# Statistics ahead of fusion's additions, no weight pieces in the fourth tile's slot, sequence 1 turned a slot later

## The chip, the cores and the metric

The kernel runs on one core of one Trainium2 chip. The metric is the device time of one execution in microseconds (us); lower is better. A kernel's time is the median of its runs. The engines are PE (TensorE: matmuls and transposes), PEld (its weight loads), DVE (VectorE), ACT (ScalarE), POOL (GpSimd) and SP (SyncE, which issues most DMAs). Each works through its own queue of instructions and waits on semaphores for the others.

## The reference: what is computed

`x` has 8 sequences of 512 tokens with 512 features, float32. A two-direction stack of four gated linear recurrences with layernorms, a fusion matmul of both directions, a residual, and a feed-forward block with ternary weights and a second residual:

```python
def _mingru(x, Wz, bz, Wh, bh):                  # here Wz and Wh are the same matrix, ctx[i]
    z = sigmoid(x @ Wz.T + bz)
    h_tilde = tanh(x @ Wh.T + bh)
    a = clip(1.0 - z, 1e-8, 1.0 - 1e-8)
    return linear_scan(a, z * h_tilde)           # h[t] = a[t] * h[t-1] + b[t], along the tokens

def _stack(x, ...):                              # 4 layers
    h = x
    for i in range(4):
        h_new = _mingru(h, ...)
        if i > 0:
            h_new = h_new + h
        h = layernorm(h_new) * gamma + beta
    return h

def _L0_xcond_ref(x, ...):
    h_fwd = _stack(x, ...)
    h_bwd = flip(_stack(flip(x), ...))
    return concat(h_fwd, h_bwd) @ fusion_W.T + fusion_b

def _L0_ffn_ref(x, ...):
    h = gelu(x @ absmean(W_fc).T)                # weights rounded to -1, 0, 1 by their mean size
    return (layernorm(h) * ln_w + ln_b) @ absmean(W_proj).T

x = x + _L0_xcond_ref(layernorm(x), ...)
x = x + _L0_ffn_ref(layernorm(x), ...)
```

## The kernel before

**Tiling and stages.** Features lie on the 128 partitions in `NC_` = 4 chunks (index `o` or `c`), tokens along the free axis; a tile is 128x512. Tokens are also cut into `NT` = 4 tiles of 128 (index `t`). The sequences are worked in four pairs (0,1), (2,3), (4,5), (6,7); a state is named by sequence and direction: (0,0), (0,1), (1,0), (1,1). A pair goes through a first layer (`first_layer`, both directions from one matmul), layers 1 to 3 (`layer`) and the fusion (`fusion`). The first layer of the next pair is woven into the fusion of this one. When all pairs are through, the feed-forward block (L747 on) runs over the eight sequences.

**Slots set the order.** The program is written in slots (`slot`, L407). A slot emits one piece of matmul work, then work that has become due, and counts `now` up by one. In a slot stand, in order: the matmuls (`work()`), the `factors` that are due, shares of the queued layernorm work (`shares`, L243, and `x_shares`), the `scans` that are due (clip L452, product L453, two scans L457), the rest of the slot's own work (`end()`), the `resid` work that is due, and last the parts of the shares that run on ACT. With `long=True`, used for the fusion tiles, `scans` and `end()` stand ahead of the shares. Within each engine the instructions keep this order.

**The layernorm between layers** (`norm`, L325) takes a token tile at a time: four transposes of 128x128 into a PSUM tile `pt` (L301; `ps_t` has two buffers), statistics on DVE (`stats`, L153: bn_stats, bn_aggr and two small operations), a power on POOL (L163), and on ACT the factor `nmr` (L173) and the normalised tile `tok` (L174), whose end frees `pt`. When the four `tok` of a state are there, `back` (L305) turns them back chunk by chunk into `pf` (two buffers) and ACT writes the new state (L316). `norm`'s argument `pause` says how many slots after the scans the first transposes come, `pair` how many go into a slot. In layer 3 (`norm_last`) only the statistics are made, and bn_stats frees `pt`.

**The fusion** (`fusion`, L535) of one token tile: DVE adds the bias `fb` to the row (L545), weight pieces are taken (`pieces`, L546), eight matmuls go into two PSUM tiles `pu` (L551; `ps_u` has four buffers, shared with `u`), and in `end()` DVE scales and adds both to the row (L559) and SP stores it (L562).

**Weight pieces.** `extra` is a list of small jobs: sums of absolute weights on ACT, the ternary weights `fcq` and `pwq` on DVE (`ternary`, L176: two operations a piece, L178 and L179), and four operations for the tile `comb` (L624 and L625). `pieces(n)` takes the next `n` of them; each piece's load is issued on SP up to three pieces ahead. They are spread over layers (L526) and fusion tiles (L546).

## Time and profile before

| | |
|---|---|
| median of 3 runs | 1749.28 us (1748.78 to 1749.43) |
| the profiled execution | 1748.87 us, its span 1746.9 us |
| mean granted TensorE clock | 0.994 of full speed |
| fusion's additions (L559) | 64, median 750 ns |
| bn_stats of a transposed tile (L156) | 256, mean 693 ns |
| scan (L457), forms `z` | 224, mean 1224 ns |
| first matmul of a first layer | 11.8 us |
| fusion of pairs 0 to 3 | from 274, 579, 884 and 1192 us |
| feed-forward block | from 1251 us |

The span runs from the first to the last instruction; the execution's time has 2.0 us more around it. A line of the timeline is: start, duration, engine, source line, operation, output<-inputs, sizes and count, and in brackets how long the engine had been idle before and what it waited for. A line of the waits is: who waited for whom, the total in us, how often, the longest. A line of a stretch is: its bounds, its length, the busy time of PE, PEld, DVE, ACT and POOL with the number of instructions, the granted clock, the share of the DMA engines and their GB/s.

### The profile page before, as it was taken

To read this page: it belongs to the slowest core of one execution; us is meant where nothing else is said; L and a number is where in the kernel's file an instruction comes from. 1 tells how busy PE (TensorE), PEld (TensorE's weight loads), DVE (VectorE), ACT (ScalarE), POOL (GpSimd) and SP (SyncE) were. 2 spreads that over 40 slices of the span, in tenths; PEclk is the share of its full clock that TensorE was granted. 3 is DMA by queue.
4 is the path that set the end of the run, shared out by engine and by line. 5 is a ranking of instruction groups with operands and counts; after the bars stand their busy time and mean duration, and the time that the engine had idled before them with its cause. 6 is when DMAs were issued, how large, how long until landed. Compare 5 with 4: busy or idle time off the path is not lost.

```text
span 1746.9 us, 19727 instructions
## 1 busy us (share of the span) xinstructions
PE 1713.6 (98%) x6424; PEld 1043.8 (60%) x6424; DVE 1453.2 (83%) x2865; ACT 1067.8 (61%) x1836; POOL 217.1 (12%) x334
## 2 busy tenths in 40 slices
PE   8899999999999989999999999999999999999998
PEld 4455554455555445555544555554588888888887
DVE  7889989779998987999898799997468778768876
ACT  3788873358886235888623588871256556565654
POOL 2011111111111111111111111111000000000000
PEclk9999999999999999999999999999999999999999
DMA  7002321150000125000012301101301101101100
GB/s 265 13 25 78 103 80 48 61 192 1 1 7 24 49 67 193 1 1 7 25 49 66 109 1 49 73 1 43 127 0 49 42 7 49 49 1 49 49 19 31
DMA packets 46454, 91.73 MB, mean 53 GB/s; under 512 B 5264, under 2 KB 5264, under 8 KB 45328
## 3 DMA queue, kind: packets, MB, share of 16 engines
q1 hardware_dynamic: 45488, 88.91, 15.1%
q10 hardware_dynamic: 864, 1.57, 0.3%
q8 instruction: 50, 0.82, 0.2%
q14 instruction: 52, 0.43, 0.1%
HBM read 65.30 MB, written 25.17 MB: 52 GB/s over the span
## 4 chain that ended last, share of the span: by engine, by line
PE 72%; DVE 21%; issue 4%; ACT 2%; POOL 0%; DMA 0%; DVEq 0%; POOLq 0%; ACTq 0%
PE u L429 27%; PE ph L790 12%; PE po L817 11%; PE pu L551 9%; DVE z L457 5%; PE pt L301 4%; PE pf L310 4%; DVE st L156 3%; DVE z L453 2%; PE u L472 2%; DVE zf L457 1%; DVE a L452 1%; DVE xf L559 1%; DVE mv L158 1%; PE py L199 1%
## 5 line engine op out<-in xcount | busy, mean ns | idle before, releaser
L429 PE MATMUL u<-h,gw 128*128 128x512 f32 x768 | 345.5, 593 | 0.0
L429 PE MATMUL u<-xT,gw 128*128 128x512 f32 x768 | 345.4, 593 | 0.0
L457 DVE TENSOR_TENSOR_SCAN z<-a,z 128x512 f32<-128x512 f32 x224 | 274.2, 1224 | 7.6
L794 ACT ACTIVATE g<-ph 128x512 f32<-128x512 f32 x128 | 76.4, 597 | 242.1 <-PE ph L790 242.1
L429 PEld LDWEIGHTS u<-h,gw 128*128 128x128 f32 x768 | 138.8, 190 | 139.1 <-issue 138.6
L429 PEld LDWEIGHTS u<-xT,gw 128*128 128x128 f32 x768 | 138.7, 190 | 139.1 <-issue 138.2
L446 ACT ACTIVATE a<-u,ngb 128x512 f32<-128x512 f32 x192 | 131.6, 685 | 141.4 <-PE u L429 140.8
L163 POOL TENSOR_TENSOR rs<-ve,mhalf 128x1 f32<-128x1 f32 x192 | 123.5, 643 | 736.4 <-DVE nmu L167 679.1
L156 DVE BATCH_NORM_STATS2 st<-pt 128x6 f32<-128x512 f32 x256 | 177.3, 693 | 33.4 <-PE pt L301 33.2
L817 PE MATMUL po<-pwq,ghi 128*128 128x512 f32 x512 | 203.6, 398 | 0.0
L790 PE MATMUL ph<-yhi,fcq 128*128 128x512 f32 x512 | 199.8, 390 | 0.0
L817 PE MATMUL po<-pwq,glo 128*128 128x512 f32 x512 | 199.7, 390 | 0.0
L790 PE MATMUL ph<-ylo,fcq 128*128 128x512 f32 x512 | 199.5, 390 | 0.0
L453 DVE TENSOR_TENSOR z<-z,t 128x512 f32<-128x512 f32 x224 | 153.4, 685 | 8.7 <-ACT z L448 8.6
L174 ACT ACTIVATE tok<-pt,nmr,rs 128x512 f32<-128x512 f32 x192 | 149.2, 777 | 6.4
L805 DVE TENSOR_TENSOR acc<-acc,g 128x512 f32<-128x512 f32 x112 | 77.3, 691 | 87.9 <-ACT g L794 87.0
L448 ACT ACTIVATE z<-u,gb 128x512 f32<-128x512 f32 x192 | 132.2, 688 | 0.0
L447 ACT ACTIVATE t<-u,gb 128x512 f32<-128x512 f32 x192 | 130.7, 681 | 0.7 <-DVE z L453 0.6
L301 PEld LDWEIGHTS pt<-ident,z 128*128 128x128 f32 x640 | 78.8, 141 | 80.5 <-issue 49.0
L173 ACT ACTIVATE nmr<-nmu,rs 128x1 f32<-128x1 f32 x192 | 56.7, 295 | 103.7 <-POOL rs L163 101.2
L551 PE MATMUL pu<-fw,xT 128*128 128x512 f32 x256 | 119.6, 611 | 0.0
L310 PE MATMUL pf<-ident,tok 128*128 128x128 f32 x768 | 113.5, 273 | 2.5 <-ACT tok L174 2.3
(138 smaller groups left out, 2621.0 us busy)
## 6 DMA issues: line engine op xcount, KB each, us to landing
xn<-in_x_dram SPq DMA_DIRECT2D x32, 256.0 KB, 4.6
xf<-in_x_dram SPq DMA_DIRECT2D x32, 256.0 KB, 5.5
x<-xf SPq DMA_DIRECT2D x32, 256.0 KB, 2.0
xy<-x SPq DMA_DIRECT2D x32, 256.0 KB, 3.7
out_dram<-xy SPq DMA_DIRECT2D x32, 256.0 KB, 2.0
xT<-in_xt_dram SPq DMA_DIRECT2D x7, 1024.0 KB, 7.3
fca<-in_fc_wT_dram SPq DMA_DIRECT2D x16, 256.0 KB, 2.9
pwa<-in_proj_wT_dram SPq DMA_DIRECT2D x16, 256.0 KB, 2.7
```

What stands on the lines that cost most here:

```text
L156: nc.vector.bn_stats(st, src)
L174: nc.scalar.activation(dst, src, AF.Identity, bias=nmr, scale=rs)
L301: nc.tensor.transpose(pt[:, ts(c, P)], zs[c][:, ts(t, P)], ident)
L310: nc.tensor.transpose(pf[:, ts(t, P)], toks[t][:, ts(c, P)], ident)
L429: nc.tensor.matmul(u, lhsT=gw[l][:, c, ts(o, P)], rhs=h[:, c, :], start=(c == 0), stop=(c == NC_ - 1),)
L446: nc.scalar.activation(a, u, AF.Sigmoid, bias=ngb[:, l, o : o + 1], scale=-1.0)
L448: nc.scalar.activation(z, u, AF.Sigmoid, bias=gb[:, l, o : o + 1])
L453: nc.vector.tensor_tensor(z, z, t, ALU.mult)
L457: nc.vector.tensor_tensor_scan(dst[:, d], a[:, d], z[:, d], 0.0, ALU.mult, ALU.add)
L551: nc.tensor.matmul(pu, lhsT=hs[d][:, c, ts(t, P)], rhs=fw[:, d * NC_ + c, :], start=(c == 0), stop=(c == NC_ - 1),)
L790: nc.tensor.matmul(ph, lhsT=w, rhs=ys[b][c][i], start=(c == 0 and i == 0), stop=(c == NC_ - 1 and i == 1),)
L817: nc.tensor.matmul(po[b][t], lhsT=part[:, ts(t, P)], rhs=pwq[k // NP_][:, k % NP_, :], start=(k == 0 and i == 0), stop=(k == NF - 1 and i ...
```

## The change

Four edits. In a `long` slot only the due `scans` stand ahead of the shares; `end()`, with fusion's two additions, now follows them as in any other slot. The last two slots of the first layers of sequences 0 and 1 become `long`. Both directions of sequence 1 wait two slots, not one, from the end of their first layer's scans to their transposes. And the pieces are dealt out differently: a fusion tile took 1, 2, 1, 2 of them; now the even sequence of a pair takes 1, 2, 1, 0 and the odd one 2, 2, 2, 2, as many in all. The four `comb` operations, which came in the four slots of state (6,0) in layer 3, now come in those of (6,1).

```diff
@@ slot
             if long:
                 due("scans")
-                end()
-                end = None
             last = shares(cap) + x_shares()
             due("scans")
             if end is not None:
@@ first_layer
-                                norm((b, 0), zf, f"{b}0_0", 1, 2 if b < 2 else 1)
+                                norm((b, 0), zf, f"{b}0_0", 2 if b == 1 else 1, 2 if b < 2 else 1)
...
-                                    norm((b, 1), zb, f"{b}1_0", 1, 2 if b < 2 else 1)
+                                    norm((b, 1), zb, f"{b}1_0", 2 if b == 1 else 1, 2 if b < 2 else 1)
@@ layer
-                if s[0] < 2 and (l == L - 1 or o % 2) and len(extra) > 2 * NW or s[0] + 2 >= B and l == L - 1:
+                if s[0] < 2 and (l == L - 1 or o % 2) and len(extra) > 2 * NW or s == (B - 2, 1) and l == L - 1:
                     pieces(1)
@@ fusion
-                    pieces(1 + t % 2)
+                    pieces((1, 2, 1, 0, 2, 2, 2, 2)[t + (b % 2) * NT])
@@ the calls of the first pair's first layers
         for i, work in enumerate(f0 + f1):
-            slot(work, 4 if i == NC_ + 1 else 2)
+            slot(work, 4 if i == NC_ + 1 else 2, i > NC_ + 1)
```

## The prediction

> **What bounds the kernel now.** First the page: how full the engines are. Then the waits of PE, then its timeline around each long wait, and last the stretches of time with their clock.

> ```profile
> span 1746.9 us, 19727 instructions
> PE 1713.6 (98%) x6424; PEld 1043.8 (60%) x6424; DVE 1453.2 (83%) x2865; ACT 1067.8 (61%) x1836; POOL 217.1 (12%) x334
> ...
> PE pt L301 <- ACT tok L174: 12.9, 8, 3.9
> PE pt L301 <- DVE zf L457: 3.9, 1, 3.9
> PE pf L310 <- ACT tok L174: 2.3, 4, 1.4
> PE pt L301 <- DVE st L156: 2.1, 6, 0.6
> ```

> PE decides the time and is idle for 33.3 us. The waits (total, times, longest) put most of it in a few places: one of 3.9 us on the last scan of sequence 1's first layer, and three of 3.9 us on a `tok`, one per fusion stage of the first three pairs. Pair 1's, in order of time:

> ```profile
> 628.53 3.60 PE L472 MATMUL u<-xT,gw 128*128 128x512 f32 x8
> 636.00 1.11 PE L301 MATMUL pt<-ident,zf 128*128 128x128 f32 x4 [3.87 <-ACT tok L174]
> 636.91 5.73 PE L551 MATMUL pu<-fw,xT 128*128 128x512 f32 x8
> ...
> 626.15 0.75 DVE L179 SCALAR_TENSOR_TENSOR fcq<-fcb,hi_fc,fcq 128x512 f32<-128x512 f32 x1
> 627.33 0.75 DVE L179 SCALAR_TENSOR_TENSOR fcq<-fcb,hi_fc,fcq 128x512 f32<-128x512 f32 x1
> 631.46 1.58 DVE L559 SCALAR_TENSOR_TENSOR xf<-pu,rsv,xf 128x512 f32<-128x512 f32 x2
> 632.95 0.69 DVE L156 BATCH_NORM_STATS2 st<-pt 128x6 f32<-128x512 f32 x1
> 634.10 0.69 DVE L156 BATCH_NORM_STATS2 st<-pt 128x6 f32<-128x512 f32 x1
> 635.17 0.78 ACT L174 ACTIVATE tok<-pt,nmr,rs 128x512 f32<-128x512 f32 x1
> ```

> The third transpose `pt` (two buffers) waits until ACT has read the first. That `tok` waits for the statistics, and DVE takes those up only at 632.95, though their `pt` stood ready by 628.3: ahead of them in its queue were two weight pieces (L178 and L179, 625.63 to 628.00), a product and two scans, and fusion's two additions (L559). The stretches show what a long wait costs besides (PE busy, PEld, DVE, ACT, POOL, then the granted clock):

> ```profile
> 631.97:636.00 4.03, 0.16 (x1) 0.00 (x0) 3.56 (x11) 1.09 (x3) 1.10 (x2) 0.80 0.41 130
> 636.00:642.47 6.47, 6.47 (x13) 3.17 (x13) 5.07 (x11) 4.07 (x7) 0.95 (x1) 0.60 0.12 43
> 1151.93:1154.00 2.07, 0.66 (x5) 0.42 (x4) 2.04 (x3) 1.29 (x3) 0.66 (x1) 1.00 0.00 0
> ```

> After a wait of 3.9 us the clock is 0.60 for 6.5 us: eight matmuls that take 3.43 us elsewhere take 5.56 (636.91 to 642.47). After the 1.4 us wait of the last pair it stays 1.00. At the start of the kernel:

> ```profile
> 46.32 0.70 DVE L156 BATCH_NORM_STATS2 st<-pt 128x6 f32<-128x512 f32 x1 [3.07 <-PE pt L301]
> 67.42 1.22 DVE L457 TENSOR_TENSOR_SCAN zf<-a,z 128x512 f32<-128x512 f32 x1
> 68.70 1.33 PE L301 MATMUL pt<-ident,zf 128*128 128x128 f32 x5 [3.88 <-DVE zf L457]
> ```

> DVE stands idle for 3.07 us before 46.32, for a transpose, with scans queued behind; 20 us later PE waits for just such a scan.

> [...] the four waits of 3.87 and 3.88 us are followed by slow matmuls, those of 1.41 us and less are not. [...] the ready statistics sat behind the additions. So position in the queue is the whole of this change. [...] Here 1224 ns against 685 for the product; two scans are the largest item moved at the start.

> **The change, part by part.** The order of instructions on each engine shows the same counts on every engine. PE's and ACT's order changes only between the end of `u_00_1_3` and the first matmuls of layer 1 of sequence 1. DVE's changes there, in the fusion slots, and in the last layer of the last pair; POOL's nowhere; on SP only three stores of x1 per pair move by a few places.

> *Fourth tile of fusion, three pairs.* DVE after the tile's addition of `fb` (ends 625.63) does no piece: clip, product and two scans, 3.46 us (628.00 to 631.46 before), end at 629.09; statistics at 629.09 and 630.24 (1.15 apart, as before), then the additions. From the start of the statistics to the end of `tok` is 3.00 us (632.95 to 635.95), so `tok` ends at 632.09. PE is through with its matmuls at 631.97 and loses 0.17. Before, it lost 10.50 (631.97 to 642.47) less 3.87 of work: 6.63; in pairs 0 and 2, 5.63 (326.77 to 336.27) and 5.62.

> *The pieces come back in the next slots* (two instead of one in tile 0 of the odd sequence; in tiles 1 and 2 two each). In that slot, after `st` for the third transpose (633.47 to 634.62), DVE does `fb` 0.60, two pieces 2.37, scans 3.46, and starts the next two statistics at 641.05 and 642.19; their `tok`s end at 644.0 and 645.14 (2.95 each, as at 646.83 to 649.78). PE, now ahead, asks for those buffers at 643.76 and 644.5: it waits 0.3 and 0.7, together 1.0, where it lost 0.31. That is 0.65 to 0.7 given back per pair. One slot on, the pieces hide under 6.87 us of fusion matmuls and a 0.12 us wait goes. The additions come 2.3 us later, ending at 632.9; the matmul that reuses their PSUM buffer starts at 636.0, so nothing waits, and 3 us of slack are left. In the last tile of the odd sequence they leave a DVE wait (2.68 us before 679.25) that covers their 1.5.

> *Tiles 0 and 2 of the even sequence.* There bn_stats alone frees `pt`; before, the third transpose waited 0.17 and 0.41 for it (pairs 1 and 2 only), plus 0.06 on each restart. With statistics first: 0.7 per pair saved.

> Pairs: 5.63-0.17-0.65+0.12 = 4.9; 6.63-0.17-0.65+0.12+0.7 = 6.6; pair 2 likewise 5.6. Sum 17.2 us.

> *The start.* With scans ahead of statistics, the clip, product and two scans of chunk 0 (3.45 us) run at 43.17 to 46.62, in the idle stretch. Statistics slip by 0.30, and PE with them once (`pf` at 51.42). DVE is 3.1 us ahead from then on; the last `zf` scan ends near 65.8 instead of 68.65. With pause 2 PE does not need it until 71.5: `pfold` and `u_01_1_0` (3.43 each) go first. Behind them come three slots in a row with two statistics each, without the 3.43 us of `pfold` between. Following DVE (2.3 for two statistics, 2.92 for clip to residual) and ACT (1.85 factors, 1.05 a `tok`, 0.7 an evacuation) slot by slot, I get PE waits of 0.65, 0.9 and 0.9, and 0.3 after. Before, between 64.33 and 99.68, PE lost 4.62 to the first transposes, 2.37 to the slow `pfold` and 0.78 in short waits: 7.8. After: 0.3+0.65+0.9+0.9+0.3 = 3.1. Gain 4.7. This term is the least sure: two engines are nearly full there (DVE 18.38 and ACT 19.05 of 20 us from 80 to 100). Bounds: 2 (waits doubled) and 7 (none).

> *Last pair.* The four `comb` pieces (1.8 us: 0.32, 0.58, 0.32, 0.60) leave sequence (6,0), and one of 0.32 precedes the statistics whose `tok` PE waited for (1.41 us). They start 1.5 earlier, at 1149.18; the wait goes, and the moved pieces add 0.1 at the next `ylo`. Gain 1.5. The FFN's statistics of `y` only profit. In fusion of sequence 6 the statistics wait for the transpose ahead of an addition that was ready, and DVE has idle time of 2.7 us per tile for it: nothing.

> The sum is 4.7+17.2+1.5 = 23.4 us. The profiled execution took 1748.87 (span 1746.9 and 2.0 around it), 0.4 below the median of 1749.28; so 1725.9, or 1726.

> **The rivals.** *B, the wait moves on.* DVE was busy nearly without a break from 625 to 643; if its lag in the slot with the two returned pieces is larger than I have it, or the start's three slots queue up, part returns as short waits: 2.5 us more per pair and 2 at the start give 1736. For it: the slack there is below 1 us. Against: DVE had 11.2 us of idle from 620 to 680, and 6.6 go.

> *C, the low clock isn't due to the wait.* Then the slow matmuls stay: 8.4 us (2.37, 1.13, 2.13, 1.12, and 0.25 plus three times 0.47 in transposes), 1734. Against: the clock is 1.00 in every stretch without such a wait.

> *D, it does not do what it says:* something else, such as ACT's turn for `tok`, held the fourth tile's slot. Then only the start's and the small gains stay, 6, and are used up by the added waits: about 1746 to 1752. Against: ACT was idle 11.0 us before that `nmr`.

> *E, slower.* Two slots in a row with two pieces, and x1 stores waiting on later additions ahead of the piece loads in SP's queue. If DVE falls 2.5 us further behind, [...] the clock falls again: about 6.5 us, at two places a pair, 39 in all against 23: 1765. [...] Against: the pieces needed are loaded a slot (8 us or more) ahead, where SP's loads landed in 2.9 us.

> **How the numbers follow.** As above 0.66 (own range 1721 to 1731), B 0.13, C 0.08, D 0.06, E 0.07. Range 1720 to 1736: below, no waits at all at the start and in the pairs; above, B and C. About 0.2% (3.5 us) is what can be told from no change. D splits over the three signs: faster 0.89, same 0.04, slower 0.07.

> **What would show it.** PE has no wait of 3.9 us after 60 us; the clock is 1.00 in the slices that had less; the `tok` of the fourth tile ends within 0.3 us of PE's last matmul; two waits near 0.3 and 0.7 us follow one slot later; before 46.6 DVE's idle of 3.07 is gone; PE's busy time falls by some 8 us and its idle time by 15. A wait above 3 us anywhere in fusion, or a clock below 1.00 there, would make it wrong.

## The result and the profile after

| | before | after |
|---|---|---|
| median of the timed runs | 1749.09 us (4 runs, 1748.78 to 1749.43) | 1724.88 us (4 runs, 1724.32 to 1725.23) |
| ratio, 95% interval | | 0.9861 (0.9844 to 0.9878) |
| span of the profiled execution | 1746.9 us | 1723.0 us |
| PE busy, PE idle | 1713.6, 33.3 us | 1704.6, 18.4 us |

24.2 us were gained, 23.4 forecast. The page of the kernel after, its span and how full the engines are:

```profile
span 1723.0 us, 19728 instructions
PE 1704.6 (99%) x6424; PEld 1039.2 (60%) x6424; DVE 1452.1 (84%) x2865; ACT 1067.0 (62%) x1836; POOL 214.6 (12%) x334
```

PE lost 14.9 us of idle time, and for the same 6424 matmuls 9.0 us of busy time. That fits the matmuls that ran at a granted clock of 0.50 before: PE was busy for 17.4 us there, and at 1.00 the same work would take half of that, 8.7 (an estimate from the granted clocks). DVE's work is the same. PE's waits (total, times, longest):

```profile
PE pt L301 <- ACT tok L174: 4.3, 11, 0.6
PE pm L669 <- DMA gw<-in_gru_wT_dram: 5.0, 1, 5.0
```

The line for `zf` is gone. The longest wait on a `tok` is 0.6 us, where it was 3.9. The 5.0 us is the first load, as before. (After line 413 every line number is two lower than before; in the experiments it is off by a few lines too.) The stretches, whose first number after the engines' busy times is the granted clock:

```profile
60.00:80.00 20.00, 19.41 (x58) 9.25 (x57) 19.09 (x38) 13.43 (x26) 1.75 (x3) 1.00 0.09 27
...
620.00:640.00 20.00, 19.06 (x62) 9.33 (x61) 18.91 (x45) 11.94 (x21) 4.09 (x6) 1.00 0.33 106
...
940.00:960.00 20.00, 20.00 (x69) 10.50 (x68) 15.63 (x25) 7.36 (x11) 0.55 (x1) 1.00 0.35 118
```

All are at 1.00. What is left of the places of the forecast stands in PE's timeline: the start, the fourth tile of pair 1 and the slot behind it, and the last pair.

```profile
76.65 0.66 PE L301 MATMUL pt<-ident,zf 128*128 128x128 f32 x4 [0.59 <-ACT tok L174]
77.14 3.60 PE L427 MATMUL u<-h,gw 128*128 128x512 f32 x8
...
617.02 3.60 PE L470 MATMUL u<-xT,gw 128*128 128x512 f32 x8
621.03 0.66 PE L301 MATMUL pt<-ident,zf 128*128 128x128 f32 x4 [0.41 <-ACT tok L174]
621.52 3.60 PE L549 MATMUL pu<-fw,xT 128*128 128x512 f32 x8
624.96 3.60 PE L549 MATMUL pu<-fw,h 128*128 128x512 f32 x8
...
634.05 0.66 PE L301 MATMUL pt<-ident,z 128*128 128x128 f32 x4 [0.48 <-ACT tok L174]
...
1129.18 0.75 PE L310 MATMUL pf<-ident,tok 128*128 128x128 f32 x4
...
1134.85 0.66 PE L199 MATMUL py<-ident,tok_y 128*128 128x128 f32 x4 [0.61 <-DVE ylo L205]
```

The third transpose of the fourth tile now loses 0.6 us to the tokens (621.52 less 617.02, less 3.43 and 0.43 of work), where the same sum gave 4.5 before (636.91 less 628.53), and `pu` behind it takes 3.44 us (621.52 to 624.96). One slot later about 1 us is lost, in all three pairs alike. In the last pair `pf` runs through, and `ylo` holds the next `py` for 0.61 us.

At the start DVE now fills the 3.07 us in which it stood idle. Its timeline has the first chunk's scan and the last `zf` scan, and no wait of DVE between 38 and 72 us:

```profile
44.09 1.22 DVE L455 TENSOR_TENSOR_SCAN zf<-a,z 128x512 f32<-128x512 f32 x1
...
64.12 1.22 DVE L455 TENSOR_TENSOR_SCAN zf<-a,z 128x512 f32<-128x512 f32 x1
```

That last scan ends at 65.34, where it ended at 68.64 before and 65.8 was forecast.

### The profile page after: what moved, and what is told of

Its sections match the earlier page's. It is cut to its first block, busy times and chain, and to the rows that moved or that the text cites. A ratio compares the mean times of both kernels' runs of the same rounds, so it can differ in the third digit from the quotient of the medians.

```text
span 1723.0 us, 19728 instructions
## 1 busy us (share of the span) xinstructions
PE 1704.6 (99%) x6424; PEld 1039.2 (60%) x6424; DVE 1452.1 (84%) x2865; ACT 1067.0 (62%) x1836; POOL 214.6 (12%) x334
## 4 chain that ended last, share of the span: by engine, by line
PE 75%; DVE 19%; issue 4%; ACT 1%; POOL 0%; DMA 0%; DVEq 0%; POOLq 0%
PE u L427 29%; PE ph L788 12%; PE po L815 12%; PE pu L549 9%; PE pt L301 5%; DVE z L455 4%; PE pf L310 4%; PE u L470 3%; DVE st L156 3%; DVE z L451 2%; DVE zf L455 1%; DVE a L450 1%; DVE mv L158 1%; PE py L199 1%; DVE z L514 1%
## 5 line engine op out<-in xcount | busy, mean ns | idle before, releaser
L427 PE MATMUL u<-xT,gw 128*128 128x512 f32 x768 | 345.4, 592 | 0.0
L455 DVE TENSOR_TENSOR_SCAN z<-a,z 128x512 f32<-128x512 f32 x224 | 274.1, 1224 | 7.6
L156 DVE BATCH_NORM_STATS2 st<-pt 128x6 f32<-128x512 f32 x256 | 177.1, 692 | 40.3 <-PE pt L301 39.8
L174 ACT ACTIVATE tok<-pt,nmr,rs 128x512 f32<-128x512 f32 x192 | 149.2, 777 | 6.4
L301 PEld LDWEIGHTS pt<-ident,z 128*128 128x128 f32 x640 | 78.4, 141 | 82.4 <-issue 47.5
L549 PE MATMUL pu<-fw,xT 128*128 128x512 f32 x256 | 115.2, 593 | 0.0
L549 PE MATMUL pu<-fw,h 128*128 128x512 f32 x256 | 115.1, 592 | 0.0
L470 PE MATMUL u<-xT,gw 128*128 128x512 f32 x256 | 114.6, 593 | 0.3 <-DVE gw L672 0.3
```

Source lines behind the costliest of these rows:

```text
L156: nc.vector.bn_stats(st, src)
L174: nc.scalar.activation(dst, src, AF.Identity, bias=nmr, scale=rs)
L301: nc.tensor.transpose(pt[:, ts(c, P)], zs[c][:, ts(t, P)], ident)
L427: nc.tensor.matmul(u, lhsT=gw[l][:, c, ts(o, P)], rhs=h[:, c, :], start=(c == 0), stop=(c == NC_ - 1),)
L455: nc.vector.tensor_tensor_scan(dst[:, d], a[:, d], z[:, d], 0.0, ALU.mult, ALU.add)
L470: nc.tensor.matmul(u, lhsT=gw[0][:, c, ts(o, P)], rhs=xT[b][:, c, :], start=(c == 0), stop=(c == NC_ - 1),)
```

## The experiments

Each change stands as a short diff against the kernel named. Ratios are to the kernel before, run on the same chip beside it.

### The two fusion edits apart and together

The order of the slot alone, from the kernel before:

```diff
             if long:
                 due("scans")
-                end()
-                end = None
```

> The kernel before with the new order of the slot alone (statistics ahead of fusion's additions); the two pieces stay in the fourth tile's slot. My theory: two thirds of the gain of the fusion slots. In the fourth tile the statistics start 1.49 us earlier (631.46 instead of 632.95 in pair 1), so the third transpose waits 2.4 us instead of 3.9; [...] the slow matmuls (1.1, 2.1 and 1.1 us) go as well, and the 0.31 us one slot later too: 3.4 + 5.1 + 4.1 = 12.6 us, 1736.5. Rival one, the clock's fall is not tied to the length of the wait: the waits shorten, the slow matmuls stay, about 1.5 + 0.7 a pair, 1743. Rival two, the order alone does it all and the dealing is not needed: 1732 and no wait over 0.5 us in the fourth tile.

The dealing of the pieces alone, from the kernel before:

```diff
-                    pieces(1 + t % 2)
+                    pieces((1, 2, 1, 0, 2, 2, 2, 2)[t + (b % 2) * NT])
```

> The kernel before with the new dealing of the pieces alone; the additions stay ahead of the statistics. My theory: the fourth tile's wait falls from 3.9 to about 1.6 us without a low clock (saves 4.85 in pair 1, 3.85 in pairs 0 and 2), but one slot later two pieces and the additions (2.37 and 1.49) stand ahead of the statistics, and two waits of about 1.7 and 0.4 us appear where 0.31 was lost: 7.5 us in all, 1741.6, less than the order alone. Rival: the additions there are covered as they are with the order changed, the give back is 0.65 a pair, and the dealing alone gives 11 us, 1738.

Both together:

> The kernel before with both fusion edits (order and dealing), the start and the last layer as before. My theory: 17.2 us, 1731.9, less than the sum of the two alone (12.6 + 7.5 = 20.1)[...]. At 20 us after the start the waits of 3.9 us (zf) and the low clock behind it stay. Rival: the start's lead of DVE carries into the fusion slots and part of their gain comes from it; then this gives clearly less, 10 to 14 us, 1735 to 1739.

| | time | ratio, 95% | gain |
|---|---|---|---|
| order alone | 1737.7 | 0.9939 (0.9927 to 0.9952) | 10.6 |
| dealing alone | 1739.43 | 0.9948 (0.9934 to 0.9961) | 8.9 |
| both | 1731.04 | 0.9902 (0.9889 to 0.9916) | 17.3 |

(kernel before in these runs: 1748.3). Both together give what was forecast for the pairs, 17.2 us, and less than 10.6 and 8.9 in sum: each alone takes a part of the same wait. Neither does it alone. That the start feeds into the fusion slots is out: the start was left as before here.

The order alone fell 2 us short of the expectation, and its timeline of PE shows why. Pair 0, then pair 1:

```profile
328.88 0.66 PE L301 MATMUL pt<-ident,zf 128*128 128x128 f32 x4 [2.36 <-ACT tok L174]
329.37 5.29 PE L549 MATMUL pu<-fw,xT 128*128 128x512 f32 x8
334.50 2.74 PE L549 MATMUL pu<-fw,h 128*128 128x512 f32 x6
...
631.82 0.66 PE L301 MATMUL pt<-ident,zf 128*128 128x128 f32 x4 [2.77 <-ACT tok L174]
632.32 3.60 PE L549 MATMUL pu<-fw,xT 128*128 128x512 f32 x8
635.75 3.60 PE L549 MATMUL pu<-fw,h 128*128 128x512 f32 x8
```

The waits are shorter, as expected. But behind the shorter of the two, 2.36 us, `pu` takes 5.13 us (329.37 to 334.50), and behind 2.77 us it takes 3.43. The longer of these two waits is not the one with the slow matmuls behind it. The dose runs below, in which spare DVE work lengthens a wait step by step, take this up.

The dealing alone did better than my 7.5. The timeline of its pair 1:

```profile
631.11 0.66 PE L301 MATMUL pt<-ident,zf 128*128 128x128 f32 x4 [1.51 <-ACT tok L174]
...
643.91 0.65 PE L301 MATMUL pt<-ident,z 128*128 128x128 f32 x4 [0.96 <-ACT tok L174]
644.98 0.65 PE L301 MATMUL pt<-ident,z 128*128 128x128 f32 x4 [0.42 <-ACT tok L174]
```

The fourth tile's wait is 1.51 (1.6 expected); one slot later 0.96 and 0.42, where I had 1.7 and 0.4.

### The start, whole and in halves

Both edits of the start, from the kernel before (in `slot`, `end` is called only where there is one):

```diff
-                                norm((b, 0), zf, f"{b}0_0", 1, 2 if b < 2 else 1)
+                                norm((b, 0), zf, f"{b}0_0", 2 if b == 1 else 1, 2 if b < 2 else 1)
...
-                                    norm((b, 1), zb, f"{b}1_0", 1, 2 if b < 2 else 1)
+                                    norm((b, 1), zb, f"{b}1_0", 2 if b == 1 else 1, 2 if b < 2 else 1)
...
-            slot(work, 4 if i == NC_ + 1 else 2)
+            slot(work, 4 if i == NC_ + 1 else 2, i > NC_ + 1)
```

> The kernel before with both edits of the start alone (second sequence turned a slot later, scans ahead of the statistics in the last two slots of the first layers). My theory: 4.7 us as forecast, 1744.4, with three waits of 0.6, 0.6 and 0.3 us at 76 to 88 us and the clock at 1.00 from 60 to 80. Rival one: it gives 5.6, as the new waits are nothing but what was lost in short waits before, 1743.5. Rival two: the lead is lost again later in layer 1 and less than 2 us is left, over 1747.

The last line of this diff alone:

> The kernel before with scans ahead of statistics in the last two slots of the first layers, and sequence 1 still turned one slot after its scans (pause 1). My theory: DVE's 3.1 us of idle time is filled, the last zf scan ends near 65.3, and the first transposes, asked for at 64.2 to 64.8, wait for it about 1 us instead of 3.9; the clock stays at 1.00, pfold takes 3.43 and stays between the statistics: 7.8 us lost before, about 2 now, 5.7 us faster, 1742.6. So this half carries the start and the pause adds nothing. Rival: the pause is what removes the wait, and without it DVE's lead is used up by the scans of the next chunk: a wait over 2 us stays, and less than 3 us is gained, over 1745.

The two `norm` lines alone:

> The kernel before with sequence 1 turned a slot later (pause 2) and nothing else. My theory: no wait for zf and no low clock (its scan ends at 68.65, the transposes come at 71), but DVE is 3.1 us later than in the changed kernel and nearly full until 88 us, so the three waits of 0.6, 0.6 and 0.3 grow by about 1.8 us in sum, to 3.3: about 4.3 us faster, 1744.0. Rival: the whole 3.1 us comes back as one wait over 2.5 us at 76 us, and the gain is below 3 us, over 1745.3.

| | time | ratio, 95% | gain |
|---|---|---|---|
| both halves | 1743.31 | 0.9971 (0.9961 to 0.9982) | 5.0 of 1748.3 |
| scans ahead alone | 1744.16 | 0.9971 (0.9959 to 0.9982) | 4.5 of 1748.66 |
| later turn alone | 1747.95 | 0.9995 (0.9987 to 1.0003) | 0.7 of 1748.66 |

Putting the scans ahead of the statistics carries the start. My expectation for it held within 1.2 us. Its timeline of PE has the short wait on `zf` and no slow `pfold`:

```profile
65.40 0.77 PE L301 MATMUL pt<-ident,zf 128*128 128x128 f32 x5 [0.71 <-DVE zf L458]
66.00 3.60 PE L635 MATMUL pfold<-fw,both 128*128 128x512 f32 x8
```

For the later turn alone my 4.3 us was wrong and the rival right. Its timeline of PE:

```profile
79.32 2.36 PE L301 MATMUL pt<-ident,zf 128*128 128x128 f32 x8 [3.03 <-ACT tok L174]
81.47 5.63 PE L429 MATMUL u<-h,gw 128*128 128x512 f32 x8
86.94 1.04 PE L301 MATMUL pt<-ident,z 128*128 128x128 f32 x8
```

The wait for `zf` did not go; it became a wait of 3.03 us for a `tok` two slots later, with its own low clock (0.50 from 78.72 to 85.55 us): eight transposes in 2.15 us (79.32 to 81.47) instead of 0.87, eight matmuls in 5.47 instead of 3.43. Moving PE's request back, without filling DVE's idle time, moves the wait. On top of the other half the later turn is worth about half a microsecond: up to the first `u` of sequence 1's layer 1 (94.61 with scans ahead alone, with 1.74 us of transposes more done, and 92.33 in the changed kernel) it is 0.5. The times cannot tell that from nothing, but the traces agree on it: from the first `u` of the first layer to the first `pu`, four kernels with both halves (the changed one, both halves alone and the two dose runs) take 256.82 to 256.85 us, and scans ahead alone 257.37.

### The comb pieces

```diff
-                if ... or s[0] + 2 >= B and l == L - 1:
+                if ... or s == (B - 2, 1) and l == L - 1:
```

> The kernel before with the four comb pieces moved from the first to the second direction's last layer of the last pair, and nothing else. My theory, now with the trace of the changed kernel: the wait of 1.41 us on a tok goes, the wait for ylo grows from 0.27 to 0.61, so 1.1 us faster, 1747.6; too little to tell by the time alone, so the two waits in its trace decide. Rival: another wait takes its place there and nothing is gained.

1747.18 us, ratio 0.9992 (0.9984 to 1.0). The trace decides, as said: the 1.41 us is gone, and the wait for `ylo` is 0.61. The second in its PE timeline:

```profile
1156.46 0.66 PE L199 MATMUL py<-ident,tok_y 128*128 128x128 f32 x4 [0.61 <-DVE ylo L205]
```

### How much lag brings the clock down

In the changed kernel, in the slot that got the pieces back:

```diff
                     pieces((1, 2, 1, 0, 2, 2, 2, 2)[t + (b % 2) * NT])
+                    if t == 0 and b % 2:
+                        for _ in range({1: 5, 3: 7, 5: 9}.get(b, 0)):
+                            nc.vector.tensor_scalar(fb, fb, 1.0, None, ALU.mult)
```

> The changed kernel with a spare multiplication of fb by 1.0 put into the first tile of the odd sequence on DVE, 5, 7 and 9 times in pairs 0, 1 and 2 (0.42 us each, so 2.1, 2.9 and 3.75 us), in the slot where two waits of 0.5 us stand. My theory (rival E of the forecast): the first of those waits grows by the added time, to 2.6, 3.4 and 4.2 us; [...] pair 0 shows 1.00, pair 2 about 0.6 for 6 us[...]; 8.8 us of waits and 1 to 4.5 us of slow matmuls, 1735 to 1738. Rival: DVE has slack there that the waits do not show, the waits grow by less than two thirds of what is added, and no clock falls.

One run, 1738.75 us, a little above what was expected. The first waits were 2.21, 3.15 and 4.06 us, as expected within 0.4. But the clock fell in all three pairs. Pair 0, in PE's timeline:

```profile
335.50 0.66 PE L301 MATMUL pt<-ident,z 128*128 128x128 f32 x4 [2.21 <-ACT tok L174]
336.64 0.71 PE L301 MATMUL pt<-ident,z 128*128 128x128 f32 x4 [0.49 <-ACT tok L174]
```

Cutting the stretches finely finds the two moments at which the granted clock changes, and with them cut there the view reads (PE's busy time is the second number, the clock the third from the end):

```profile
333.70:337.11 3.41, 1.12 (x8) 0.89 (x9) 3.23 (x8) 2.36 (x5) 1.10 (x2) 1.00 0.01 3
337.11:340.52 3.41, 3.41 (x9) 1.91 (x8) 3.09 (x11) 3.34 (x6) 1.50 (x2) 0.50 0.53 153
340.52:343.93 3.41, 3.41 (x9) 1.52 (x8) 3.34 (x6) 1.08 (x3) 0.00 (x0) 1.00 0.55 191
```

The clock is at 0.50 for 3.41 us. In pair 1 it falls at 640.90, in pair 2 at 944.68: 303.79 us and 303.78 us apart, 89 times the 3.41 us of a low stretch (303.79 over 89 is 3.413). The pairs themselves come about 304 us apart in this run, so equal distances alone say little. But in the kernel before the four falls, at 67.74, 330.57, 634.35 and 941.55 us, are 262.83, 303.78 and 307.20 us apart, and these are 77, 89 and 90 times 3.413. What sets these moments, the runs do not show. A second dose run, with 3, 5 and 6 multiplications, had these distances in its theory:

> As the dose kernel, with the spare multiplication 3, 5 and 6 times in pairs 0, 1 and 2. By the first dose run the first wait should be 1.3, 2.2 and 2.7 us, with 0.5 behind it. Theory one, [...] any fall of the clock begins and ends at times that lie whole multiples of 3.41 us apart, lasts 3.41 or 6.83 us, and comes where over half to two thirds of the stretch before it was idle (above 1.64, at most 2.25 us); pair 0 keeps 1.00, pairs 1 and 2 fall or not as the wait lies in one stretch or across two. [...] About 1730 to 1734.

One run, 1733.98 us. The waits came to 1.30, 2.22 and 2.68 us, each with 0.5 behind it. The clock kept 1.00 in pair 0 and fell in the others, at 637.38 and 941.17, again 303.79 apart, each time for 3.41 us. The stretches of 3.41 us before and after (pair 0's begins 303.78 us, 89 times 3.413, ahead of pair 1's fall):

```profile
333.60:337.01 3.41, 1.88 (x13) 1.54 (x14) 3.13 (x10) 3.00 (x6) 0.55 (x1) 1.00 0.23 82
633.97:637.38 3.41, 1.03 (x7) 0.79 (x8) 3.23 (x10) 2.26 (x5) 1.10 (x2) 1.00 0.00 0
637.38:640.80 3.42, 3.42 (x10) 2.08 (x9) 3.10 (x11) 3.35 (x6) 1.50 (x2) 0.50 0.49 156
937.76:941.17 3.41, 1.13 (x8) 0.90 (x9) 3.23 (x8) 2.37 (x5) 1.10 (x2) 1.00 0.01 3
```

That is as the first theory had it: PE was busy for 1.03 and 1.13 us of the stretches ahead of the two falls, and for 1.88 us where the clock stayed at 1.00. The length of one wait does not tell the two apart: the falls stand behind 2.22 and 2.68 us here, and the order alone kept 1.00 behind 2.77. Its trace, cut in the same way: pair 0 at its fall, at 330.05 us, and then, from 87 times 3.413 us later, the two stretches over which the wait of its pair 1 is spread:

```profile
326.64:330.05 3.41, 1.18 (x6) 0.88 (x7) 3.13 (x10) 2.15 (x4) 1.10 (x2) 1.00 0.00 0
330.05:333.46 3.41, 3.41 (x5) 1.35 (x4) 3.23 (x10) 3.04 (x5) 0.95 (x1) 0.50 0.58 154
627.01:630.42 3.41, 2.04 (x5) 0.57 (x3) 3.23 (x7) 0.00 (x0) 0.34 (x1) 1.00 0.24 90
630.42:633.83 3.41, 2.01 (x8) 1.26 (x9) 3.20 (x9) 2.76 (x5) 0.76 (x2) 1.00 0.12 44
```

The wait of 2.36 us lies nearly whole in one stretch and leaves PE 1.18 us busy there, and the next is at 0.50; the wait of 2.77 us is split, each stretch keeps 2.0, and the clock stays at 1.00.

### Can it be done better?

The changed kernel with one piece instead of two in the first tile of the odd sequence, and the comb pieces in the last layer of sequence 7's forward direction instead of sequence 6's backward one:

```diff
-                    pieces((1, 2, 1, 0, 2, 2, 2, 2)[t + (b % 2) * NT])
+                    pieces((1, 2, 1, 0, 1, 2, 2, 2)[t + (b % 2) * NT])
...
-                if ... or s == (B - 2, 1) and l == L - 1:
+                if ... or s == (B - 1, 0) and l == L - 1:
```

> The changed kernel with two placements altered: one piece instead of two in the first tile of the odd sequence (dealing 1 2 1 0 1 2 2 2, eleven a pair, ten in the third), and the comb pieces in the third instead of the second direction's last layer of the last pair. My theory: in the slot after the fourth tile DVE has 1.19 us less ahead of the statistics, both waits there (0.49 and 0.48) go in all three pairs, 2.9 us; the wait of 0.61 for ylo goes, and the slot it moves to takes four pieces of 0.3 to 0.6 with under 0.3 of slack each, so at most 0.6 is gained or as much lost there: 3 us in all, ratio to the kernel before 0.9845 (1722). Rival: the pieces that are dealt later put the same delay into a later slot, and the time is that of the changed kernel, 1724.9 or a ratio of 0.9862.

1721.5 us (1720.79 to 1721.81), ratio 0.9844 (0.983 to 0.9858). Against the changed kernel's 0.9861 the intervals overlap, so the trace decides: its span is 1719.3 us against 1723.0, and it shows both waits after the fourth tile gone in all three pairs, and the wait for `ylo` down from 0.61 to 0.36. Pair 1, in PE's timeline, runs through:

```profile
627.65 3.60 PE L470 MATMUL u<-xT,gw 128*128 128x512 f32 x8
631.09 1.19 PE L301 MATMUL pt<-ident,z 128*128 128x128 f32 x8
```

On top of it I tried to spread sequence 1's backward statistics at the start:

```diff
-                                    norm((b, 1), zb, f"{b}1_0", 2 if b == 1 else 1, 2 if b < 2 else 1)
+                                    norm((b, 1), zb, f"{b}1_0", 2 if b == 1 else 1, 2 if b < 1 else 1)
```

> The version with eleven pieces a pair (v_a) and, on top, the backward statistics of sequence 1 one per slot instead of two. My theory: the waits of 0.60 and 0.27 us at 81 and 87 us go, the one of 0.59 at 76 stays; 0.9 us below v_a, ratio to the kernel before 0.984 (1720.6). Rival: the statistics then come in the slots with layer 1's residual additions, the same waits appear there or the second pair of sequences is ready too late and a slot stands empty; no faster than v_a, or several us slower.

1721.6 us, ratio 0.9846 (0.9832 to 0.9859), and the same three waits: 0.59, 0.59 and 0.27. The edit did next to nothing. By the program this is because `shares` takes a second piece where one is overdue, and behind the forward direction's four these always are; no run tests that alone. So the same with pause 4, to make them due later:

> The version v_a with sequence 1's backward statistics one per slot and due two slots later (pause 4), so that the queue does not take them as late, two at a time. My theory: of the three slots at 75 to 88 us with two statistics each the two for z get one each; PE lost 0.91 and 0.50 us there, and both go, 0.91 for zf stays: 1.4 us below v_a, 1720.1, ratio 0.9836. Rival: DVE and ACT are nearly full until 120 us, and the statistics that now come beside those of layer 1's first sequences wait there; the same 1.4 us is lost later, 1721.5 (0.9844) or a little more.

1724.61 us, ratio 0.9861 (0.9844 to 0.9877). The interval overlaps with that of the version without it, but the traces show it slower: from the first `u` of the first layer to the first `pu` it takes 260.07 us against 256.83, and the stretches behind that are alike. The last two of the three waits shrink to one of 0.27, but sequence 1's backward direction is then ready too late, and its layer 1 waits for it:

```profile
111.47 0.66 PE L310 MATMUL pf<-ident,tok 128*128 128x128 f32 x4 [1.77 <-ACT h L316]
...
114.41 1.98 PE L427 MATMUL u<-h,gw 128*128 128x512 f32 x4 [0.56 <-ACT h L316]
```

Neither of my two theories for this run had that; the rival of the run before it had named it. The version with eleven pieces a pair has the lowest time of this study, level with its first variant.

## Why the prediction was right, point by point

- **The pairs: 17.2 forecast, 17.3 measured** with both fusion edits alone. The mechanism was as put: position in DVE's queue. In the traces of the kernel before and the changed one, pairs 0 to 2 are shorter by 4.9, 6.5 and 5.8 us (4.9, 6.6 and 5.6 forecast). That the sum fits so closely is partly luck, as two small misses cancel. The fourth tile's loss came to 0.2, 0.6 and 0.3 us in the three pairs (0.17 forecast); in pair 1 `tok` ends 0.5 us after PE's last matmul, not within 0.3, because within the pair PE comes there 1.0 us earlier than before and DVE only 0.6 (in pair 2 0.9). Against that, tiles 0 and 2 of pair 1 gave 1.0 us, not 0.7: from the first `pu` to the fourth tile's `u` it was 50.03 us (578.50 to 628.53) and is 49.02 (568.00 to 617.02). What is lost one slot later is 0.97 us per pair, 1.0 forecast, as two waits of 0.5 and not 0.3 and 0.7.
- **The start: 4.7 forecast, 5.0 measured.** The three slots lost 0.91, 0.91 and 0.50 us, 2.3 in all (77.14 less 71.93, less 3.43 and 0.87, and so on), where I had 3.1 with the two small ones; the 0.3 at `pf` did not come. So the term was 0.8 too small: from the first `u` to the first `pu` the changed kernel is 5.5 us shorter (11.78 to 274.09 before, 11.66 to 268.51 after). The kernel with both halves alone shows less of it because in its trace the three fusion stages, left as they were, take 0.6 us more than before (the end shows how such stages vary). What I did not work out is that one half carries it: the later turn alone gave 0.7 (0.9987 to 1.0003).
- **The last pair: 1.5 forecast, 1.5 measured** by the difference of medians (1748.66 less 1747.18), at the edge of what can be told. In the trace it is 1.1: 1.41 gone, and 0.34 more at `ylo`, not 0.1.
- The parts add up: 17.3, 5.0 and 1.5 are 23.8, against 24.2 for the whole. In the forecast's sum of 23.4 the start was too small and the last pair too large, which brings the total nearer than its parts.
- **Rival B** (waits move on) is not seen: behind pair 1's fusion PE's one wait up to pair 2 is 0.23 us (675.84), and the kernel before has the same one (692.81). **Rival C** (low clock not due to the wait) is out: with the waits shortened by nothing but the order of instructions the slow matmuls went from pairs 1 and 2 (behind waits of 2.77 and 2.46 us `pu` took 3.43 and 3.44), and with added waits they came back (0.50 for 3.41 us in each pair of the first dose run). **Rival D** is out by the fourth tile's timeline.
- **Rival E was mis-sized.** How much lag brings the clock down the trace of the kernel before did not show: there it stayed at 1.00 behind 1.41 us and fell behind 3.87. It fell with 5 multiplications, 2.1 us of lag at 0.426 us each in the first dose run, and not with 3 (1.3 us). And a place cost less than 6.5 us: from the start of `u` to the second `pu`, pairs 0 to 2 of the first dose run took 13.01, 13.79 and 14.31 us against 9.14 without, so 3.9, 4.7 and 5.2 us. The rival did not occur, but 2.1 us of further lag would have been enough for the clock.

## What to carry to other kernels

- When the engine that feeds the deciding one has work queued ahead of a ready instruction, as DVE had here, move what nothing waits for (pieces, additions with slack) behind that instruction (17.3 us here); then price what the moved work delays one slot later.
- Moving the consumer's request later gains little unless the producer's idle time is filled as well: here the later request alone gave 0.7 us, which is within the noise, filling the idle time alone 4.5, both 5.0.
- Here the clock fell behind a wait of 2.22 us with one of 0.5 us after it (PE busy for 1.03 of the 3.41 us before the fall), and not behind one of 2.77 us: the length of the longest wait alone gave too wide a margin.

## What the runs showed of the hardware

```profile
329.34:332.76 3.42, 2.84 (x7) 1.81 (x8) 2.04 (x6) 3.32 (x6) 0.89 (x2) 0.50 0.14 37
...
629.72:633.13 3.41, 1.36 (x4) 0.29 (x2) 3.17 (x8) 0.00 (x0) 0.00 (x0) 1.00 0.09 34
633.13:636.54 3.41, 1.58 (x5) 1.25 (x6) 2.03 (x7) 2.64 (x5) 1.10 (x2) 0.50 0.46 127
...
109.22:112.63 3.41, 1.64 (x11) 1.12 (x10) 3.20 (x9) 2.82 (x6) 0.66 (x1) 1.00 0.02 5
```

In the second dose run's stretch from 333.60 to 337.01, behind which the clock stayed at 1.00, transposes make up nearly all of PE's 1.88 us: `pu` starts at 336.72 and has 0.29. The kernel before at its start, cut at its fall:

```profile
64.33:67.74 3.41, 0.49 (x4) 0.25 (x2) 3.31 (x6) 2.78 (x7) 0.00 (x0) 1.00 0.24 77
67.74:71.15 3.41, 2.45 (x7) 1.80 (x8) 3.34 (x5) 0.95 (x2) 0.00 (x0) 0.50 0.00 0
71.15:74.57 3.42, 3.42 (x5) 1.35 (x4) 3.23 (x7) 0.00 (x0) 0.53 (x1) 0.50 0.00 0
```

PE is busy 0.49 us in the first, and the second is at 0.50; the second still has 0.96 us of the wait in it, and the third is at 0.50 too. Waits of the same length, 3.87 us, cost 1.1 us of slow matmuls in pairs 0 and 2 of the kernel before, where the clock was low for 3.41 us, and 2.1 in pair 1, where it was low for 6.83. The times of kernels that keep such waits also scatter more (both edits of the start: 1741.19 to 1745.46, against 0.9 us between the changed kernel's). The later turn alone leaves fusion as it was: there the clock was low for 3.41 us in pair 1 and 6.83 in pair 2, the other way round, and from its first `pu` to the next pair's, pair 1 took 304.74 us (305.83 in the kernel before) and pair 2 308.77 (307.63). And of the seven runs of both edits of the start the fastest has the highest mean clock, 0.998, the slowest the lowest, 0.995, and the five between have 0.996.
